# Latents' attention over a context: a new order of transposes, divisions and value products within a batch

## The chip, the cores and the metric

The kernel runs on one core of a Trainium2 chip. The core has five engines that work side by side: TensorE (PE in the profile; its weight loads are listed as PEld), VectorE (DVE), ScalarE (ACT), GpSimd (POOL) and SyncE (SP), which only issues transfers here. Each engine takes its instructions in order, and an instruction waits on semaphores for what other engines produce. The metric is the time of one execution on the device, in microseconds; the lower the better.

## The reference, cut to what matters

The whole kernel is a network of twelve blocks in float32 on x of 16 x 64 tokens by 256. The change is in the tenth block, an attention of the latents (the layer-normed x) over a context of 1024 tokens and over the latents themselves, with a mask on the context:

```python
xn = layernorm(x, ln_x_g, ln_x_b)              # the context, 16 x 1024 x 192
ln = layernorm(latents, ln_l_g, ln_l_b)        # 16 x 64 x 256
q = ln @ Wq.T
kv = jnp.concatenate([xn @ Wkv.T, ln @ Wlkv.T], axis=1)
k, v = (kv[..., :INNER], kv[..., INNER:])      # INNER = 256: 4 heads of 64
...
qn = rmsnorm(q, qn_g) * SCALE
kn = rmsnorm(k, kn_g)
attn = jnp.einsum('bhid,bhjd->bhij', qn, kn)
attn = jnp.where(full_mask[:, None, None, :], attn, -jnp.finfo(attn.dtype).max)
attn = jax.nn.softmax(attn, axis=-1)
out = jnp.einsum('bhij,bhjd->bhid', attn, v)
out = out.transpose(0, 2, 1, 3).reshape(b, m, INNER)
return out @ Wo.T + bo
```

## The kernel before, in words

The block is `xattn3` (L1448 on). It loops over the 16 batches of 64 queries each. The four heads are two pairs, c = 0 and 1, and a pair's scores lie in one tile of 128 rows (two heads by 64 queries) and 1152 keys: 1024 of the context and 128 columns for the latents, half of them masked. Softmax runs along these 1152 keys.

The loop is pipelined over two batches. While batch b is scored, divided and multiplied with its values, the keys and values of batch b + 1 are made. They come in four pieces of 256 context keys (`project`, L1553): products on PE, then four evictions by DVE that apply the context's normalisation, two for keys (`kk`) and two for values (`vv`). Each piece's keys then need their own norm: `square` on ACT, `roots` (a sum by DVE, and two POOL instructions, L1522 and L1523), `scale` on DVE, and `keys_T` (L1583): four transposes on PE into one PSUM accumulator and one copy from there to `kT`. The latents' own keys and values (`latents`, L1538) are a product for two batches at once, so it runs in every second batch; the keys go the same way through square, roots and scale.

For batch b itself: `scores` on PE for the first 512 keys, for the latents' and for the other 512; `least` on DVE adds the mask and keeps the running minimum (the gain has a negative sign); one exponential on ACT per pair gives probabilities `prs[c]` and their sums; a reciprocal on DVE and a multiplication on ACT divide them. Then the probabilities are transposed, eight blocks of a pair by `probs_T` (L1624, two accumulators, two ACT copies into `pT`) and the latents' block of both pairs by `last_T` (L1593), which in this version also transposes the latents' keys of the next batch in the same accumulator. `values` (L1631) multiplies 36 small products per pair into one accumulator `po`, ACT copies `po` to `oT`, and every second batch `output` (L1643) multiplies the output weights for an earlier pair of batches and DVE adds the result to X.

What sets the order is the text of the loop. Between `set_order(True)` and `set_order(False)` every instruction on PE, and every one issued through the wrapped `dve` and `act` queues, is chained to the one before it on its engine, so these three engines run in just the order in which the loop's lines stand. POOL's instructions and the transfers are placed by a scheduler. In the profile the chained DVE and ACT instructions all carry the line of the wrapper, L72, products L188 and transposes L191, so a reader tells them apart by tile names: `pkv` a projection, `ptk` a piece's key transposes, `ptl` those of `last_T`, `ptp` those of `probs_T`, `pss` scores, `po` values or output, `rnk` the norm's sums and roots.

PSUM holds seven accumulators for all of these (`mid`) and one for `po`. The first batch's keys are made ahead of the loop; batches 1 to 3 also make the queries of four later batches each (`queries`, `queries_T`), and batch 0 normalises the second half of the latents.

Of the kernel before, what the change touches and what calls it, by code (L numbers as in the profile page):

```python
# [8 lines left out]
F32 = mybir.dt.float32  # L9
# [6 lines left out]
P = 128  # L16
# [3 lines left out]
S, C = 1024, 192  # L20
C1 = C - P
NKC = S // P
# [56 lines left out]
class Net:  # L79
# [1368 lines left out]
    def xattn3(self):  # L1448
# [9 lines left out]
        H, KT = 4, NKC + 1  # L1458
# [4 lines left out]
        with ExitStack() as es:  # L1463
# [2 lines left out]
            dram = es.enter_context(tc.tile_pool(name=f"{L}dram", bufs=1, space=bass.MemoryType.DRAM))  # L1466
            mid = es.enter_context(tc.tile_pool(name=f"{L}mid", bufs=7, space=PSUM))
            ps_o = es.enter_context(tc.tile_pool(name=f"{L}ps_o", bufs=1, space=PSUM))
            if not hasattr(self, "wx"):
                self.context_weights()(mid)  # L1470
            wx, bx = self.wx, self.bx


# [37 lines left out]
            def square(x, n):  # L1511

                sq = two.tile([P, 2 * H, 64], F32, tag="sq", name="sq")
                act.activation(sq[:, : n * H].rearrange("p (j h) d -> p j h d", j=n), x, AF.Square)
                return x, n, sq

            def roots(x, n, sq):

                rn = self.small.tile([P, 2 * H], F32, tag="rnk", name="rnk", bufs=6)
                r = rn[:, : n * H]  # L1520
                dve.tensor_reduce(r, sq[:, : n * H], AX.X, ALU.add)
                nc.gpsimd.tensor_scalar(r, r, 1.0 / 64, 1e-16, ALU.mult, ALU.max)  # L1522
                nc.gpsimd.tensor_tensor(r, r, self.mhalf[:, : n * H], ALU.pow)  # L1523
                return x, r.rearrange("p (j h) -> p j h", j=n)

            def scale(x, r):
                dve.tensor_tensor(x, x, bc(r, 3, 64), ALU.mult)
# [25 lines left out]
            def project(b, j):  # L1553

                c0, c1 = ctxs[b]
                kk, vv = kks[b % 2], vvs[b % 2]
                pp = [mid.tile([P, 512], F32, tag="m", name="pkv") for _ in range(2)]
                for n in range(2):
                    jj = 4 * n + j
                    self.mm(pp[n], c0[:, jj * P : (jj + 1) * P], wx[:, 0, :], True, False)  # L1560
                for n in range(2):
                    r = slice(n * 64, (n + 1) * 64)
                    self.mm(pp[n], c1[r, j * P : (j + 1) * P], wx[r, 1, :], False, True)
                for n in range(2):
                    for i, dst in enumerate((kk, vv)):
                        jj = 4 * n + j
                        dve.scalar_tensor_tensor(
                            dst[:, 2 * j + n].rearrange("p h d -> p (h d)"),
                            pp[n][:, i * D : (i + 1) * D],
                            self.rctx[:, b, jj : jj + 1],  # L1570
                            bx[:, i * D : (i + 1) * D],
                            ALU.mult,
                            ALU.add,
                        )
                return kk[:, 2 * j : 2 * j + 2], 2

            def turn(pt, at, x):
                self.tr(pt[:, at * P : (at + 1) * P], x)

            def pair(b, k, c):  # L1580
                return kks[b % 2][:, k, 2 * c : 2 * c + 2, :].rearrange("p h d -> p (h d)")

            def keys_T(b, j, copy):  # L1583

                if j == 0:
                    st["kT"] = one.tile([P, 2, KEYS], F32, tag="kT", name="kT")
                pt = mid.tile([P, 512], F32, tag="m", name="ptk")
                for c in range(2):
                    for n in range(2):
                        turn(pt, 2 * c + n, pair(b, 2 * j + n, c))  # L1590
                copy(st["kT"][:, :, 2 * j * P : 2 * j * P + 2 * P], pt.rearrange("p (c k) -> p c k", c=2))

            def last_T(b, keys, prs):  # L1593

                pt = mid.tile([P, 512], F32, tag="m", name="ptl")
                if keys:
                    for c in range(2):
                        turn(pt, c, pair(b, NKC, c))
                if prs:
                    st["pT"] = one.tile([P, 2, KT, P], F32, tag="pT", name="pT")  # L1600
                    for c in range(2):
                        turn(pt, 2 + c, prs[c][:, S:])
                    act.copy(st["pT"][:, :, NKC, :], pt[:, 2 * P :].rearrange("p (c q) -> p c q", c=2))
                if keys:
                    act.copy(st["kT"][:, :, S:], pt[:, : 2 * P].rearrange("p (c k) -> p c k", c=2))

            def scores(b, lo, hi):

# [15 lines left out]
            def probs_T(c, pr):  # L1624
                for jh in range(2):
                    pt = mid.tile([P, 512], F32, tag="m", name="ptp")
                    for j in range(4):
                        turn(pt, j, pr[:, (4 * jh + j) * P : (4 * jh + j + 1) * P])
                    act.copy(st["pT"][:, c, 4 * jh : 4 * jh + 4, :], pt.rearrange("p (j q) -> p j q", q=P))
# [79 lines left out]
            p0 = roots(*p0)  # L1709
# [17 lines left out]
            late = square(*late)  # L1727
            scale(*lat)
            keys_T(0, 2, act.copy)
            last_T(0, True, None)  # L1730
            late = roots(*late)
            scale(*late)
            norm(1)
            for b in range(B):
                more = b + 1 < B
                load(b + 2)
                load_off(b + 1)
                prs = [two.tile([P, KEYS], F32, tag="pr", name="pr") for _ in range(2)]
                nms = [3e38, 3e38]
                sums = self.small.tile([P, 2], F32, tag="sums", name="sums")  # L1740
                st["po"] = ps_o.tile([P, 2 * TQ], F32, tag="o", name="po")
                pss = scores(b, 0, 512)
                for c in range(2):
                    least(b, pss, 0, 512, prs, nms, c)
                keys_T(b, 3, act.copy)
                if more:
                    lat = latents(b + 1)
                    p0 = square(*project(b + 1, 0))
                    lat = square(*lat)
                psl = scores(b, S, KEYS)  # L1750
                pss = scores(b, 512, S)
                for c in range(2):
                    least(b, psl, S, KEYS, prs, nms, c)
                    least(b, pss, 512, S, prs, nms, c)
                    act.activation(prs[c], prs[c], AF.Exp, bias=nms[c], scale=-1.0, accum_out=sums[:, c : c + 1])
                if more:
                    p0, lat = roots(*p0), roots(*lat)
                    p1 = project(b + 1, 1)
                    scale(*p0)
                dve.reciprocal(sums, sums)  # L1760
                if more:
                    p1 = square(*p1)
                act.mul(prs[0], prs[0], sums[:, 0:1])
                if more:
                    p1 = roots(*p1)
                if 1 <= b <= 3:
                    q = queries(b)
                if b == 0:
                    normed(1)
                if more:  # L1770
                    p2 = project(b + 1, 2)
                    scale(*p1)
                    scale(*lat)
                    if b == 0:
                        norm_T(1)
                    keys_T(b + 1, 0, act.copy)
                act.mul(prs[1], prs[1], sums[:, 1:2])
                if 1 <= b <= 3:
                    q = roots(*q)
                if more:  # L1780
                    p2 = roots(*square(*p2))
                    late = project(b + 1, 3)
                last_T(b + 1, more, prs)
                probs_T(0, prs[0])
                if more:
                    late = square(*late)
                    keys_T(b + 1, 1, dve.tensor_copy)
                    late = roots(*late)
                    scale(*p2)
                if 1 <= b <= 3:  # L1790
                    scale(*q)
                probs_T(1, prs[1])
                values(b, 0)
                if more:
                    keys_T(b + 1, 2, dve.tensor_copy)
                if 1 <= b <= 3:
                    queries_T(b, q[0])
                if b % 2 == 0 and b > 0:
                    output(b // 2 - 1)
                values(b, 1)  # L1800
                if more:
                    scale(*late)
                act.copy(oT[:, :, b * TQ : (b + 1) * TQ], st["po"].rearrange("p (c q) -> p c q", c=2))
                if 1 <= b <= NT:
                    nc.gpsimd.tensor_tensor(self.X[:, b - 1, :], self.X[:, b - 1, :], row, ALU.add)
# [771 lines left out]
```

## Time and profile before

| | |
|---|---|
| median of three runs | 3303.53 us |
| lowest and highest | 3290.88 and 3317.2 us |
| the profiled execution: time | 3300.39 us |
| the profiled execution: span | 3298.7 us |
| mean granted TensorE clock over the span | 0.959 |
| busy PE / DVE / ACT / POOL over the span | 94 / 56 / 37 / 22 % |
| the latents' attention's batches | about 2622 to 3007 us |

The span runs from the first to the last instruction; the time has 1.7 us more around it. A row of a group gives line, engine, operation, the tile written and the tiles read, shapes and the number of instructions; then busy time. In a timeline the first two numbers are start and length in us, and a bracket tells how long the engine was idle before and which instruction released it. A row of a stretch gives each engine's busy time with its count of instructions, then the granted clock of TensorE (1.00 is full speed), the share of busy DMA engines and GB/s. A row of waits gives who waited for whom, us in total, times, and the longest.

### The profile page before, as it was taken

What the parts mean: (1) busy time and instruction counts of PE and PEld (TensorE: products, weight loads), DVE (VectorE), ACT (ScalarE), POOL (GpSimd) and SP (SyncE); (2) the same over time, 40 slices, a digit from 0 to 9 for tenths busy, and PEclk for the clock granted to TensorE, in tenths of its full rate; (3) what the DMA queues carried; (4) which work ended last, traced back from release to release, by engine and by line L of the source; (5) the groups of instructions that cost most, each with busy time, mean ns of one, the idle gap of its engine ahead of it and who ended that gap; (6) DMA issues with size and microseconds to landing.
All of it is one profiled execution on the core that took longest, in us unless ns stands there. A gap on an engine that the chain in (4) does not pass through costs nothing.

```text
span 3298.7 us, 48631 instructions
## 1 busy us (share of the span) xinstructions
PE 3085.0 (94%) x20064; PEld 1753.1 (53%) x20064; DVE 1857.1 (56%) x3497; ACT 1213.9 (37%) x2093; POOL 723.5 (22%) x786
## 2 busy tenths in 40 slices
PE   7999999999999999979969999998999899998787
PEld 4666665664344344468834434434665454455676
DVE  6888885424444445961135545557884677775521
ACT  3555554213322221003322232228861254544211
POOL 1000003311200001014410000023771354441131
PEclk9999999999999999969989999998998999999889
DMA  2100000012122113027821111101111111110233
GB/s 71 32 29 30 31 24 11 20 48 79 58 76 73 59 38 78 20 84 288 294 89 58 49 52 54 48 17 34 45 52 34 64 61 55 58 51 14 83 110 118
DMA packets 64511, 213.63 MB, mean 65 GB/s; under 512 B 16433, under 2 KB 27556, under 8 KB 57378
## 3 DMA queue, kind: packets, MB, share of 16 engines
q1 hardware_dynamic: 37296, 106.13, 9.6%
q0 software_dynamic: 21840, 99.39, 9.0%
q10 hardware_dynamic: 5154, 5.01, 0.5%
q8 instruction: 159, 2.61, 0.3%
q14 instruction: 62, 0.51, 0.1%
HBM read 201.62 MB, written 12.66 MB: 65 GB/s over the span
## 4 chain that ended last, share of the span: by engine, by line
PE 78%; DVE 8%; issue 5%; POOL 5%; ACT 3%; DMA 1%; POOLq 0%; DVEq 0%; SPq 0%; ACTq 0%
PE pss L188 14%; PE o L188 13%; PE pst L191 8%; PE pu L188 6%; PE psp L188 5%; PE pd L188 5%; PE py L188 4%; PE psc L188 3%; POOL rnk L1523 2%; PE po L188 2%; PE pb L191 2%; PE psq L188 1%; PE pkv L188 1%; DVE pr L72 1%; DVE kk L72 1%
## 5 line engine op out<-in xcount | busy, mean ns | idle before, releaser
L72 DVE TENSOR_REDUCE nm<-pss 128x1 f32<-128x1024 f32 x256 | 307.4, 1222 | 349.6 <-PE pss L188 349.6
L72 ACT COPY pT<-pst 128x512 f32<-128x512 f32 x256 | 149.8, 585 | 688.8 <-PE pst L191 688.5
L188 PE MATMUL pss<-cT,qw 128*128 128x512 f32 (+1 forms) x1024 | 387.8, 628 | 1.6 <-ACT qw L72 1.6
L188 PE MATMUL o<-pT,cx 128*128 128x512 f32 (+1 forms) x1024 | 370.5, 606 | 0.0
L191 PEld LDWEIGHTS pst<-ident,pr 128*128 128x128 f32 x2048 | 219.8, 141 | 159.1 <-issue 100.1
L72 ACT ACTIVATE pr<-pss,nm 128x1024 f32<-128x1024 f32 x256 | 285.1, 1114 | 34.4 <-DVE nm L72 21.0
L191 PE MATMUL pst<-ident,pr 128*128 128x128 f32 x2048 | 281.0, 280 | 5.7 <-DVE v L72 1.6
L188 PEld LDWEIGHTS pss<-cT,qw 128*128 128x128 f32 (+1 forms) x1024 | 125.8, 187 | 251.1 <-issue 239.4
L188 PEld LDWEIGHTS o<-pT,cx 128*128 128x128 f32 (+1 forms) x1024 | 112.6, 162 | 166.3 <-issue 145.0
L72 DVE TENSOR_SCALAR pr<-pr,sm 128x1024 f32<-128x1024 f32 x256 | 193.1, 754 | 9.0
L188 PE MATMUL pkv<-wx,cT 128*128 128x512 f32 (+1 forms) x512 | 190.2, 623 | 0.6 <-issue 0.6
L205 POOL TENSOR_SCALAR rs<-mv 128x8 f32<-128x8 f32 (+3 forms) x53 | 10.2, 193 | 802.3 <-DVE mv L221 400.3
L72 DVE COPY pT<-pst 128x512 f32<-128x512 f32 x256 | 174.5, 682 | 8.6 <-PE pst L191 4.5
L72 DVE TENSOR_TENSOR_SCAN h<-dA,pb 128x512 f32<-128x512 f32 x128 | 154.7, 1217 | 15.9 <-PE pb L191 9.0
L1347 POOL TENSOR_TENSOR h<-h,cb 128x1024 f32<-128x1024 f32 x64 | 151.4, 2367 | 53.3 <-DVE h L72 51.3
L188 PE MATMUL pd<-wd,hT 128*128 128x256 f32 x656 | 149.3, 382 | 3.0 <-DVE hT L2391 1.4
L2203 DVE TENSOR_SCALAR y<-pd,row 128x256 f32<-128x256 f32 x39 | 18.9, 484 | 223.7 <-PE pd L188 223.7
L188 PEld LDWEIGHTS pd<-wd,hT 128*128 128x128 f32 x656 | 123.1, 190 | 31.3 <-DVE hT L2391 6.2
L1523 POOL TENSOR_TENSOR rnk<-rnk,mhalf 128x8 f32<-128x8 f32 (+1 forms) x84 | 130.2, 1550 | 7.0
L188 PE MATMUL py<-h,ident 128*128 128x512 f32 x256 | 131.1, 598 | 0.0
L188 PEld LDWEIGHTS pu<-xT,up 128*128 128x128 f32 x736 | 110.8, 192 | 21.8 <-ACT hT L2197 14.6
L188 PE MATMUL pu<-xT,up 128*128 128x128 f32 x736 | 121.2, 290 | 1.1 <-DVE xT L2189 0.5
(511 smaller groups left out, 5195.6 us busy)
## 6 DMA issues: line engine op xcount, KB each, us to landing
cT<-in_ctxT SPq DMA_DIRECT2D x64, 768.0 KB, 4.4
cx<-in_ctxP SPq DMA_DIRECT2D x32, 768.0 KB, 4.3
offb<-d_off SPq DMA_DIRECT2D x16, 576.0 KB, 3.7
cb<-d_C SPq DMA_DIRECT2D x16, 512.0 KB, 3.6
wu<-in_L_ffn_w POOLq DMA_DIRECT2D x8, 1024.0 KB, 5.7
wd<-in_L_ffn_w POOLq DMA_DIRECT2D x8, 1024.0 KB, 6.3
wc<-in_L_attn_conv_wT POOLq DMA_DIRECT2D x4, 1024.0 KB, 10.2
T<-d_T SPq DMA_DIRECT2D x8, 512.0 KB, 18.5
```

The lines of the kernel that those rows point to most:

```text
L72: ins = getattr(self.engine, op)(*args, **kwargs)
L188: self.in_order(self.nc.tensor.matmul(out, lhsT=lhsT, rhs=rhs, start=start, stop=stop))
L191: self.in_order(self.nc.tensor.transpose(out, in_, self.ident))
L205: nc.gpsimd.tensor_scalar(t[:p, :n], in_, scale, eps, ALU.mult, ALU.add)
L1347: nc.gpsimd.tensor_tensor(hs[i], hs[i], cbs[hf, g], ALU.mult)
L1523: nc.gpsimd.tensor_tensor(r, r, self.mhalf[:, : n * H], ALU.pow)
L2203: nc.vector.tensor_scalar(y[:, i, :], po[:, i * D : (i + 1) * D], weight[:, g + i : g + i + 1], None, ALU.mult)
```

## The change: what it does

It rewrites the order within a batch.

- The first piece's key transposes (`keys_T(b + 1, 0)`) move from between the third and fourth projection to behind the fourth and behind the first pair's probabilities.
- `last_T` is split: `latents_T` for the next batch's latents' keys, and `last_T` for the latents' block of the probabilities. Each has its own accumulator and stands at its own place, the keys' one late, ahead of piece 1's transposes.
- The reciprocal of both sums becomes two, one per pair. The first division stands right after the first reciprocal, ahead of piece 1's projection in the text; the second right after piece 1's square.
- Scalings on DVE move: piece 0's behind the second reciprocal, piece 1's behind the fourth piece's eviction.
- The copies of pieces 1 and 2 move from DVE to ACT.
- Both value products stand together; piece 2's transposes, the queries' transposes and the output product come after them.
- A branch that builds the context's weights, if no earlier block has done so, is removed; the ninth block does so (L2354).

```diff
--- before.py
+++ after.py
@@ -1466,8 +1466,6 @@
             dram = es.enter_context(tc.tile_pool(name=f"{L}dram", bufs=1, space=bass.MemoryType.DRAM))
             mid = es.enter_context(tc.tile_pool(name=f"{L}mid", bufs=7, space=PSUM))
             ps_o = es.enter_context(tc.tile_pool(name=f"{L}ps_o", bufs=1, space=PSUM))
-            if not hasattr(self, "wx"):
-                self.context_weights()(mid)
             wx, bx = self.wx, self.bx
 
 
@@ -1590,19 +1588,19 @@
                         turn(pt, 2 * c + n, pair(b, 2 * j + n, c))
                 copy(st["kT"][:, :, 2 * j * P : 2 * j * P + 2 * P], pt.rearrange("p (c k) -> p c k", c=2))
 
-            def last_T(b, keys, prs):
+            def latents_T(b):
 
                 pt = mid.tile([P, 512], F32, tag="m", name="ptl")
-                if keys:
-                    for c in range(2):
-                        turn(pt, c, pair(b, NKC, c))
-                if prs:
-                    st["pT"] = one.tile([P, 2, KT, P], F32, tag="pT", name="pT")
-                    for c in range(2):
-                        turn(pt, 2 + c, prs[c][:, S:])
-                    act.copy(st["pT"][:, :, NKC, :], pt[:, 2 * P :].rearrange("p (c q) -> p c q", c=2))
-                if keys:
-                    act.copy(st["kT"][:, :, S:], pt[:, : 2 * P].rearrange("p (c k) -> p c k", c=2))
+                for c in range(2):
+                    turn(pt, c, pair(b, NKC, c))
+                act.copy(st["kT"][:, :, S:], pt[:, : 2 * P].rearrange("p (c k) -> p c k", c=2))
+
+            def last_T(prs):
+
+                pt = mid.tile([P, 512], F32, tag="m", name="pto")
+                for c in range(2):
+                    turn(pt, c, prs[c][:, S:])
+                act.copy(st["pT"][:, :, NKC, :], pt[:, : 2 * P].rearrange("p (c q) -> p c q", c=2))
 
             def scores(b, lo, hi):
 
@@ -1727,7 +1725,7 @@
             late = square(*late)
             scale(*lat)
             keys_T(0, 2, act.copy)
-            last_T(0, True, None)
+            latents_T(0)
             late = roots(*late)
             scale(*late)
             norm(1)
@@ -1755,49 +1753,55 @@
                     act.activation(prs[c], prs[c], AF.Exp, bias=nms[c], scale=-1.0, accum_out=sums[:, c : c + 1])
                 if more:
                     p0, lat = roots(*p0), roots(*lat)
+                dve.reciprocal(sums[:, 0:1], sums[:, 0:1])
+                act.mul(prs[0], prs[0], sums[:, 0:1])
+                if more:
                     p1 = project(b + 1, 1)
-                    scale(*p0)
-                dve.reciprocal(sums, sums)
+                dve.reciprocal(sums[:, 1:2], sums[:, 1:2])
                 if more:
                     p1 = square(*p1)
-                act.mul(prs[0], prs[0], sums[:, 0:1])
+                act.mul(prs[1], prs[1], sums[:, 1:2])
                 if more:
+                    scale(*p0)
                     p1 = roots(*p1)
                 if 1 <= b <= 3:
                     q = queries(b)
                 if b == 0:
                     normed(1)
                 if more:
-                    p2 = project(b + 1, 2)
-                    scale(*p1)
+                    p2 = square(*project(b + 1, 2))
                     scale(*lat)
                     if b == 0:
                         norm_T(1)
-                    keys_T(b + 1, 0, act.copy)
-                act.mul(prs[1], prs[1], sums[:, 1:2])
                 if 1 <= b <= 3:
                     q = roots(*q)
                 if more:
-                    p2 = roots(*square(*p2))
+                    p2 = roots(*p2)
                     late = project(b + 1, 3)
-                last_T(b + 1, more, prs)
+                st["pT"] = one.tile([P, 2, KT, P], F32, tag="pT", name="pT")
                 probs_T(0, prs[0])
                 if more:
+                    keys_T(b + 1, 0, act.copy)
+                last_T(prs)
+                if more:
                     late = square(*late)
-                    keys_T(b + 1, 1, dve.tensor_copy)
+                probs_T(1, prs[1])
+                if more:
+                    scale(*p1)
                     late = roots(*late)
                     scale(*p2)
+                    latents_T(b + 1)
+                    keys_T(b + 1, 1, act.copy)
                 if 1 <= b <= 3:
                     scale(*q)
-                probs_T(1, prs[1])
                 values(b, 0)
+                values(b, 1)
                 if more:
-                    keys_T(b + 1, 2, dve.tensor_copy)
+                    keys_T(b + 1, 2, act.copy)
                 if 1 <= b <= 3:
                     queries_T(b, q[0])
                 if b % 2 == 0 and b > 0:
                     output(b // 2 - 1)
-                values(b, 1)
                 if more:
                     scale(*late)
                 act.copy(oT[:, :, b * TQ : (b + 1) * TQ], st["po"].rearrange("p (c q) -> p c q", c=2))
```

## The prediction

> **What bounds the kernel now.** I read the page first, then the stretches of the latents' attention, its waits, and the timeline of two of its batches.
>
> ```profile
> span 3298.7 us, 48631 instructions
> PE 3085.0 (94%) x20064; PEld 1753.1 (53%) x20064; DVE 1857.1 (56%) x3497; ACT 1213.9 (37%) x2093; POOL 723.5 (22%) x786
> ```
>
> TensorE (PE) is busy nearly throughout. The changed stage is 16 batches, from about 2622 to 3007 us, 12% of the span. One batch with the latents' product and one without, with columns PE, PEld, DVE, ACT, POOL and the granted clock:
>
> ```profile
> 2798.10:2822.40 24.30, 22.60 (x174) 11.45 (x176) 16.79 (x43) 12.11 (x21) 10.91 (x13) 1.00 0.17 57
> 2822.40:2845.70 23.30, 21.61 (x172) 11.20 (x172) 17.95 (x44) 11.52 (x20) 10.49 (x11) 1.00 0.19 60
> ```
>
> PE fills all but 1.7 us of each. [...] in the timeline the 512-column passes of a projection follow each other every 0.43 us (0.19 us of weight load, 0.24 us of PEld idle behind it), without a wait on another engine. The waits of PE itself in these two batches are what an order can remove:
>
> ```profile
> PE ptl L191 <- DVE kk L72: 1.9, 2, 0.9
> PE ptk L191 <- DVE sums L72: 1.0, 2, 0.5
> PE ptk L191 <- DVE kk L72: 0.5, 2, 0.3
> ```
>
> Together 3.4 us in two batches, 1.7 us in each, the same 1.7 us as 24.30 - 22.60. The timeline shows where:
>
> ```profile
> 2811.92 0.63 PE L191 MATMUL ptk<-ident,kk 128*128 128x128 f32 x4 [0.48 <-DVE sums L72]
> ...
> 2813.40 1.66 POOL L1523 TENSOR_TENSOR rnk<-rnk,mhalf 128x8 f32<-128x8 f32 x1
> ...
> 2815.09 1.03 DVE L72 TENSOR_TENSOR kk<-kk,rnk 128x512 f32<-128x512 f32 x2 [1.10 <-POOL rnk L1523]
> ...
> 2816.27 0.41 PE L191 MATMUL ptl<-ident,kk 128*128 128x128 f32 x2 [0.94 <-DVE kk L72]
> ...
> 2818.24 0.69 DVE L72 COPY kT<-ptk 128x512 f32<-128x512 f32 x1
> ...
> 2820.55 0.63 PE L191 MATMUL ptk<-ident,kk 128*128 128x128 f32 x4 [0.27 <-DVE kk L72]
> ```
>
> Piece 0's transposes come between the third and fourth projection, 0.48 us too early for their scaling. The latents' transposes wait 0.94 us because DVE scales piece 1 first, and that waits for a POOL root. Piece 2's transposes wait 0.27 us.
>
> **The change, part by part.** I lay the new order onto this batch, counting from its first score product (2798.08 = 0), with each duration from the timeline. Up to the exponentials nothing changes: last score minima at 10.13, piece 1's products start at 7.34.
>
> *PE.* Each projection takes 2.97 us (weight loads from 2805.42 to 2808.39), and now three follow without a gap: 7.34, 10.31, 13.28, end 16.25. Their accumulators come free in time: a pool of seven gives the fourth piece those of scores read by 10.1. Then comes one row of 28 transposes at 0.13 us (8 took 1.04): first probabilities to 17.3, piece 0 to 17.8, the latents' probabilities to 18.05, second probabilities to 19.05, latents' keys to 19.3, piece 1. Then both values, 1.2 us each, and piece 2.
>
> *The divisions.* ACT ends both exponentials at 11.66. The first reciprocal (at most the 0.16 us of the present two-column one) runs at 11.14 on DVE, hidden behind the second exponential, so the first division (1.25 us) runs 11.66 to 12.91; square of piece 1 (0.62) to 13.53; second division to 14.78. PE wants them at 16.25 and 17.8: covered by 3 us each. The reciprocal more per batch, 0.16 us of DVE, lies in DVE's chain below.
>
> *DVE, the chain to watch.* From 10.13: two reductions 1.01, reciprocal 0.16, eviction of piece 1 (4 by 0.39) 1.57, reciprocal 0.16; scaling of piece 0 at 13.1 (its POOL root is done at 12.97) to 13.78, reduction (0.67) to 14.45, eviction of piece 2 to 16.0, latents' scaling (0.35) to 16.4. ACT squares piece 2 by 16.4, so DVE reduces it to 17.2, evicts the fourth piece to 18.8 and scales piece 1 only now, to 19.5. PE is at piece 1's transposes at 19.35 and a signal takes 0.14 us: a wait of 0.3 us. That is the new late one. Queued behind it are both values, piece 2 and the next batch's scores. The latents' scaling was done 2.9 us before PE wants it: the 0.94 us is gone. Piece 0 is scaled 3.5 us ahead: the 0.48 us is gone.
>
> *Later steps.* Square of the fourth piece on ACT by 19.6, reduction by 20.4, scaling of piece 2 by 21.1; PE wants it at 22.5: the 0.27 us is gone. POOL's root of the fourth piece is done near 22.5, DVE scales it by 23.25, and the next batch's transposes want it at 23.9. In even batches the addition of the output to X (0.42 us) stands before that scaling, and output is now the last thing on PE: X and scaling end 1.25 us after output, PE arrives after 1.02 us of scores. I take 0.3 us of new wait in every second batch.
>
> *Copies.* Pieces 1 and 2 move from DVE (2 by 0.69) to ACT (2 by 0.58): ACT 12.1 to 13.3 of some 23 us. Between 17 and 21.7 ACT works without a gap; the second probabilities' copies are done at 20.7, their values start at 21.3. Covered with 0.6 us; if ACT were later, each us would stop the second values.
>
> *No cost.* Separating the two halves of one accumulator adds no instruction, only an accumulator of the seven. The removed branch is never taken, since an earlier block sets these weights. No DMA is moved; the context's load waits for the fourth projection, which now ends 1 us sooner in the batch. POOL keeps its five roots of 0.25 + 1.66 us or less, under 12 of 23 us.
>
> *What has no row.* Whether 28 transposes in a row hold the clock. [...] the new row lasts 3.6 to 4 us, today's longest some 2.7. This trace has a row that speaks more strongly:
>
> ```profile
> 3001.00:3002.00 1.00, 1.00 (x6) 1.00 (x6) 0.00 (x0) 0.58 (x1) 0.00 (x0) 0.50 0.00 0
> 3002.00:3002.50 0.50, 0.50 (x5) 0.50 (x3) 0.00 (x0) 0.41 (x1) 0.00 (x0) 0.50 0.00 0
> 3002.50:3003.00 0.50, 0.50 (x10) 0.29 (x11) 0.00 (x0) 0.35 (x2) 0.00 (x0) 0.97 0.00 0
> ```
>
> In the last batch, after 6 us of idle PE, only transposes run from 2999.1 to 3002.7, and at its end the clock is back at full. So they count: zero by the row. [...] with the transposes at the slow 0.21 us of that stretch another 28 x 0.08 = 2.2 us. Below nothing it can't go: the clock is at 1.00 already.
>
> **The sum.** Batches 4 to 14: 1.7 - 0.3 - 0.15 = 1.25 us each, 13.7. Batches 1 to 3 have the queries' product and lengths of 25.97, 25.11 and 26.73 us between first scores; products of 24.7, 23.9 and 24.7 (the steady 22.55 or 20.8, 0.9 for output, 2.2 for queries) leave 4.4 idle, and I take 4.1 of it, since DVE's chain has the queries' 1.7 us on PE as cover. Batch 0: PE waits for the normalised latents as before (1.4 us), later waits of some 1.7 us go, one new appears: 0.8. Last batch: division starts 0.2 us sooner, and the first probabilities' transposes no longer stand behind the second division: about 1.1. In all 19.7, say 20 us, of the profiled 3300.4 us (span 3298.7 and 1.7 around it) 0.6%. Applied to the median of 3303.5: 3283.
>
> **The rivals.**
> *DVE's chain takes the place of the removed waits.* Piece 1's scaling behind the fourth eviction has 0 us of margin. If each of DVE's dozen steps starts 0.1 us later than I laid it, it is 1.2 us later, the batch keeps a wait of 1.5 us and little is left: about 1 us in the edges and batches 1 to 3 most of 4: 3298. For it: DVE has hardly a gap from 10.1 to 19.5. Against: the steps' starts are read from the trace, with their gaps.
> *Slower: the clock falls in the row of transposes.* [...] The three rows above speak against it.
> *More than forecast.* Neither new wait appears and the contiguous values pack closer: all 1.7 us in 11 batches, 4.4, 2 in batch 0 and 2 in the last, 27 us: 3276. More than that the stage doesn't hold as idle PE.
>
> **Chances.** Forecast 0.60 (3277 to 3290), DVE's chain 0.20 (3290 to 3303), more 0.13 (3268 to 3277, with the scatter of a median), slower by the clock 0.07. About 1% is what a measurement can tell from no change here, since the three times span 0.8%. The range 3268 to 3303 takes the first three with some scatter out at either end. Faster by over 1% needs 33 us, more than the idle PE in the stage, so only scatter gives it: 0.08. Slower by over 1% [...]: 0.05. The rest, 0.87, is within 1%.
>
> **What would show it.** The period of two steady batches falls from 47.6 to about 45.1 us; the waits of the latents' keys on DVE and of piece 0 vanish from PE's list; a wait of piece 1's transposes on DVE's scaling of about 0.3 us appears; in every second batch one of the fourth piece's transposes behind output; the stage's granted clock stays 1.00. I am wrong if piece 1's wait is over 1 us (DVE), if the second values wait for ACT's copies, or if the clock in the stretch of transposes drops.

## The result, and the profile after

The changed kernel takes 3270.5 us (median of 20 runs, 3262.9 to 3292.6), the kernel before 3293.9 (median of 20, 3288.1 to 3321.9): a ratio of 0.9925 with a 95% interval of 0.9905 to 0.9946, or 23 us (18 to 31 by the interval). The profiled execution went from 3300.4 to 3274.8 us. The forecast was 20 us less, to 3283 us.

The page of the changed kernel, its span and the busy shares:

```profile
span 3273.1 us, 48693 instructions
PE 3078.7 (94%) x20064; PEld 1750.0 (53%) x20064; DVE 1837.4 (56%) x3483; ACT 1228.6 (38%) x2123; POOL 727.5 (22%) x786
```

PE's share is the same 94%, so the page alone shows nothing of where the time went. The stretches of two steady batches do, one with the latents' product and one without (columns as before: PE, PEld, DVE, ACT, POOL, granted clock, DMA share, GB/s):

```profile
2786.71:2809.50 22.79, 22.53 (x170) 11.33 (x169) 16.42 (x44) 12.26 (x21) 10.94 (x14) 1.00 0.18 61
2809.50:2831.20 21.70, 21.64 (x169) 11.21 (x168) 15.61 (x40) 13.18 (x24) 10.71 (x11) 1.00 0.20 65
```

They took 24.30 and 23.30 us before. PE's work is the same; its 1.7 us of idle time per batch is now 0.26 and 0.06. PE's own waits over batches 5 to 14 of the changed kernel are a single row, where the kernel before had three (1.7 us per batch):

```profile
PE ptk L191 <- PE pss L188: 0.9, 5, 0.2
```

This is the wait, in every second batch, of the next batch's last key transposes. The row names the scores, but DVE's scaling ends just then. Batch 4 has one wait more, of 0.48 us, for a scaling that comes late behind the last queries. The timeline of one batch of the changed kernel shows where the old waits were and the two new ones (start, length, what; in brackets the idle time ahead of it):

```profile
2786.82 0.42 DVE L72 TENSOR_TENSOR X<-X,po 128x256 f32<-128x256 f32 x1 [2.90 <-PE po L188]
2787.16 0.69 DVE L72 TENSOR_TENSOR kk<-kk,rnk 128x512 f32<-128x512 f32 x1
...
2787.99 0.63 PE L191 MATMUL ptk<-ident,kk 128*128 128x128 f32 x4 [0.19 <-PE pss L188]
...
2794.28 8.99 PE L188 MATMUL pkv<-wx,cT 128*128 128x512 f32 x24
...
2803.20 1.09 PE L191 MATMUL ptp<-ident,pr 128*128 128x128 f32 x8
...
2805.27 0.69 DVE L72 TENSOR_TENSOR kk<-kk,rnk 128x512 f32<-128x512 f32 x1
...
2805.65 0.38 PE L191 MATMUL ptl<-ident,kk 128*128 128x128 f32 x2
...
2806.10 0.63 PE L191 MATMUL ptk<-ident,kk 128*128 128x128 f32 x4
...
2806.66 2.32 PE L188 MATMUL po<-pT,vv 128*64 128x64 f32 x72
```

Three projections run as one piece of 8.9 us, followed without a gap by the row of transposes. Piece 1's (`ptk` at 2806.10) start 0.45 us after the latents' two, which take 0.22: a wait of 0.23 us. DVE ends the scaling that they need at 2805.96, and its signal takes 0.14. The list of PE's waits doesn't have this one, since the modelled end of the transposes ahead covers most of it. The output's addition to X and the scaling behind it end at 2787.85, and the transposes at 2787.99 wait for them: 0.19 us by the list.

I measure the stage from the start of its first score product to the start of its last output product: 383.5 us before, 364.7 changed. That is 18.9 us of the span's 25.6. The other 6.7 us lie outside it.

### The profile page after: what moved, and what is told of

Its sections match the earlier page's. It is cut to its first block, busy times and chain, and to the rows that moved or that the text cites. A ratio compares the mean times of both kernels' runs of the same rounds, so it can differ in the third digit from the quotient of the medians.

```text
span 3273.1 us, 48693 instructions
## 1 busy us (share of the span) xinstructions
PE 3078.7 (94%) x20064; PEld 1750.0 (53%) x20064; DVE 1837.4 (56%) x3483; ACT 1228.6 (38%) x2123; POOL 727.5 (22%) x786
## 4 chain that ended last, share of the span: by engine, by line
PE 84%; DVE 6%; issue 4%; POOL 2%; ACT 2%; DMA 1%; ACTq 0%; SPq 0%; POOLq 0%; DVEq 0%
PE pss L188 15%; PE o L188 13%; PE pst L191 8%; PE pu L188 6%; PE psp L188 5%; PE pkv L188 5%; PE pd L188 5%; PE py L188 4%; PE psc L188 3%; PE po L188 2%; PE pb L191 2%; PE psq L188 2%; PE psi L188 1%; PE psy L188 1%; PE psqw L188 1%
## 5 line engine op out<-in xcount | busy, mean ns | idle before, releaser
L2207 DVE TENSOR_SCALAR y<-pd,row 128x256 f32<-128x256 f32 x39 | 18.9, 484 | 223.9 <-PE pd L188 223.9
L188 PEld LDWEIGHTS pkv<-wx,cT 128*128 128x128 f32 (+1 forms) x512 | 64.4, 189 | 118.5 <-issue 92.2
## 6 DMA issues: line engine op xcount, KB each, us to landing
wc<-in_L_attn_conv_wT POOLq DMA_DIRECT2D x4, 1024.0 KB, 10.8
```

Of the source, the lines that this page charges most:

```text
L188: self.in_order(self.nc.tensor.matmul(out, lhsT=lhsT, rhs=rhs, start=start, stop=stop))
L2207: nc.vector.tensor_scalar(y[:, i, :], po[:, i * D : (i + 1) * D], weight[:, g + i : g + i + 1], None, ALU.mult)
```

## The experiments

All compare two steady batches (first score product to the first score product two batches later; 47.59 us before, 44.48 changed), the sum of batches 1 to 3, which also make queries, and the stage. Whole times of single runs scatter too much for this. The stage also holds the first and the last batch, whose length depends on where the clock falls in that profile (below), so a difference of one to three us between two stages says little by itself. In a_only, keys0_early, copies_dve and dve_late, the rows of waits are over eight steady batches.

| kernel (all in us) | two steady batches | batches 1 to 3 | stage |
|---|---|---|---|
| before | 47.59 | 77.81 | 383.5 |
| changed | 44.48 | 73.31 | 364.7 |
| a_only | 47.59 | 78.00 | 386.2 |
| keys0_early | 45.52 | 73.73 | 369.8 |
| p1_scaled_first | 47.31 | 75.32 | 382.1 |
| long_transposes | 50.97 | 83.25 | 416.4 |
| values_apart | 44.54 | 75.78 | 365.8 |
| copies_dve | 44.97 | 74.70 | 368.2 |
| one_division | 44.48 | 73.29 | 364.7 |
| dve_late | 45.69 | 75.04 | 372.7 |
| three_parts | 44.54 | 77.57 | 368.3 |
| warm_clock | 44.48 | 73.30 | 362.9 |
| warm_and_order | 44.35 | 73.84 | 358.4 |
| after_again | 44.48 | 73.29 | 364.7 |

**One move alone (a_only).** On the kernel before:

```diff
-                    keys_T(b + 1, 0, act.copy)
                 act.mul(prs[1], prs[1], sums[:, 1:2])
...
                     late = project(b + 1, 3)
+                    keys_T(b + 1, 0, act.copy)
                 last_T(b + 1, more, prs)
```

> The kernel before with one part of the change: piece 0's key transposes and their copy stand behind the fourth projection instead of ahead of it. Two steady batches took 47.6 us before and take 44.5 us changed. My theory, that the waits come from the order of scalings on DVE and from POOL's root: the 0.48 us wait at piece 0 goes, but the latents' transposes still need DVE's scaling of piece 1 and then of the latents, which comes no sooner, so their wait grows from 0.94 to about 1.4 us, and two batches stay at 47.6 (47.4 to 47.8). Rival, that each removed wait is a gain by itself: two batches fall by 2 x 0.48 to 46.7.

47.59 us, to the hundredth what it was. PE's waits over eight steady batches of this kernel:

```profile
PE ptl L191 <- DVE kk L72: 10.1, 8, 1.3
PE ptk L191 <- DVE kk L72: 2.2, 8, 0.3
```

The wait at piece 0 is gone and the latents' has grown from 0.94 to 1.3 us a batch. A removed wait is worth nothing while the next one on the same engine hangs on the same chain.

**That move undone (keys0_early).** On the changed kernel:

```diff
                     if b == 0:
                         norm_T(1)
+                    keys_T(b + 1, 0, act.copy)
...
                 probs_T(0, prs[0])
-                if more:
-                    keys_T(b + 1, 0, act.copy)
```

> The changed kernel with piece 0's transposes and copy back between the third and fourth projection. My theory: PE is there at about 13.5 us of the batch, and the scaling of piece 0, now behind two reciprocals, ends at 13.9 and is signalled 0.14 later, so a wait of 0.5 us comes back; the wait of 0.2 us at piece 1 goes in exchange, two batches take 45.1 (44.9 to 45.6) against 44.5. Rival, that the place of piece 0 doesn't matter because DVE's chain sets the batch: 44.5.

45.52: undoing the move loses 0.52 us a batch, where alone the move gained nothing. Its waits over eight batches:

```profile
PE ptk L191 <- DVE kk L72: 3.8, 8, 0.5
PE ptk L191 <- PE pss L188: 0.8, 4, 0.2
```

0.48 us each, at piece 0. The loss is at the upper end of what I expected.

**Piece 1's scaling put back (p1_scaled_first).**

```diff
                     p2 = square(*project(b + 1, 2))
+                    scale(*p1)
                     scale(*lat)
...
                 if more:
-                    scale(*p1)
                     late = roots(*late)
```

> The changed kernel with DVE's scaling of piece 1 back ahead of the latents' scaling, ahead of piece 2's reduction and the fourth piece's eviction; nothing else is moved. My theory: DVE waits there for piece 1's POOL root (about 0.6 us) and everything behind it, the fourth eviction, its square and its root, comes 0.6 to 1.1 us later; the second probabilities need the accumulator of the fourth piece, and the next batch's last transposes need its scaling, so two batches lose 0.8 to 2 us: 45.3 to 46.5. Rival, that separating the latents' transposes is what gained and the place of this scaling is free: 44.5, or 44.1 since the wait of 0.2 us at piece 1 goes.

47.31: this one line takes back 2.8 of the 3.1 us, more than I expected. Its timeline:

```profile
2813.15 1.66 POOL L1521 TENSOR_TENSOR rnk<-rnk,mhalf 128x8 f32<-128x8 f32 x1
...
2814.85 1.03 DVE L72 TENSOR_TENSOR kk<-kk,rnk 128x512 f32<-128x512 f32 x2 [1.17 <-POOL rnk L1521]
...
2816.78 0.47 DVE L72 SCALAR_TENSOR_TENSOR vv<-pkv,rctx,bx 128x256 f32<-128x256 f32 x1
...
2817.40 0.63 PE L191 MATMUL ptp<-ident,pr 128*128 128x128 f32 x4 [1.14 <-DVE vv L72]
```

DVE stands 1.17 us, not 0.6, behind POOL's root with the fourth piece's eviction queued behind it. The second half of the second probabilities' transposes needs the accumulator that this eviction frees, and PE waits 1.14 us for it. Without the new place of this scaling, all the rest of the change, the latents' separate transposes with it, gains 0.3 us in two batches; the rival falls.

**The row of transposes, longer (long_transposes).**

```diff
                 for c in range(2):
                     turn(pt, c, prs[c][:, S:])
+                for n in range(32):
+                    turn(pt, 2 + n % 2, prs[n % 2][:, :P])
```

> The changed kernel with 32 more transposes per batch, of blocks already transposed, into the unused half of the accumulator of the latents' probabilities; their results are not read. The row of transposes between the fourth projection and the values becomes 60 long, about 8 us. My theory, that transposes count as activity for the clock: the granted clock stays 1.00 in that row and a batch grows by 32 x 0.13 = 4.2 us, two batches 44.5 + 8.4 less 0.4 = 52.5. Rival, that they don't count: the clock falls to about half within the row, transposes take 0.21 us, and two batches take 56 us or more.

50.97: 3.24 us more a batch, less than I expected. The transposes follow each other at 0.11 us (34 from 2821.58 to 2825.29), not the 0.13 that I took from a group of eight with its tail: 3.5 us, less the wait at piece 1 that they cover. The clock is the eighth number of these rows:

```profile
2821.00:2822.00 1.00, 1.00 (x11) 1.00 (x10) 1.00 (x4) 1.00 (x3) 0.89 (x2) 1.00 0.51 123
2824.00:2825.00 1.00, 1.00 (x12) 1.00 (x11) 0.00 (x0) 0.00 (x0) 0.00 (x0) 1.00 0.05 18
2826.00:2827.00 1.00, 1.00 (x12) 0.83 (x11) 0.56 (x1) 1.00 (x3) 0.00 (x0) 1.00 0.00 0
```

From 2820.2 to 2826.9, 6.7 us, PE does transposes only, and the granted clock stays 1.00, here and in the score products behind (every us from 2820 to 2845). The slower rival of the prediction is out.

**The values apart (values_apart).**

```diff
                 values(b, 0)
-                values(b, 1)
...
                     output(b // 2 - 1)
+                values(b, 1)
```

> The changed kernel with the two value products apart again: piece 2's transposes, the queries' and the output product stand between them. Theory A, that bringing both values together removed the wait of piece 2's transposes: the 0.27 us come back, two batches take 45.0. Theory B, that DVE's scaling of piece 2 is now ready before the first values end (by 0.3 us in the changed kernel's trace): no wait returns, and the output's addition to X is no longer late, so the 0.19 us at the next batch's last transposes goes: 44.3.

44.54, between the two. No wait of PE is left in its list, so theory B is right on both waits. But the values joined take 2.25 us from the first of them to the next transposes (2806.66 to 2808.91 in the changed kernel), apart 1.20 each. The joined values are worth 0.15 us a batch, a little more than the late addition to X costs (0.2 us in every second batch). In batches 1 to 3 keeping them apart costs 2.5 us: piece 2's scaling comes later there, behind the queries' reduction and root.

**The copies on DVE (copies_dve).**

```diff
-                    keys_T(b + 1, 1, act.copy)
+                    keys_T(b + 1, 1, dve.tensor_copy)
...
-                    keys_T(b + 1, 2, act.copy)
+                    keys_T(b + 1, 2, dve.tensor_copy)
```

> The changed kernel with the copies of pieces 1 and 2 back on DVE. My theory: ACT gets shorter by 1.2 us and DVE longer by 1.4; piece 2's copy stands ahead of the fourth piece's scaling on DVE, which ends 0.6 us later, so the next batch's last transposes wait 0.5 us more in batches with output and not in the others: two batches 45.0 (44.7 to 45.4). Rival, that ACT without a gap behind the probabilities was the tighter one: at most 44.5.

44.97, with a wait of 0.5 us in every second batch, as laid out; its list over eight batches:

```profile
PE ptk L191 <- DVE kk L72: 1.8, 4, 0.5
PE ptk L191 <- PE pss L188: 0.8, 4, 0.2
```

**One late division (one_division).**

```diff
-                dve.reciprocal(sums[:, 0:1], sums[:, 0:1])
-                act.mul(prs[0], prs[0], sums[:, 0:1])
                 if more:
                     p1 = project(b + 1, 1)
-                dve.reciprocal(sums[:, 1:2], sums[:, 1:2])
+                dve.reciprocal(sums, sums)
                 if more:
                     p1 = square(*p1)
+                act.mul(prs[0], prs[0], sums[:, 0:1])
                 act.mul(prs[1], prs[1], sums[:, 1:2])
```

> The changed kernel with one reciprocal of both sums behind piece 1's eviction and both divisions on ACT behind piece 1's square. My theory: both are ready at about 16.1 us of the batch, PE wants the first at 16.5 and the second at 17.8, so the sooner division gains nothing directly; piece 2's square on ACT starts 0.3 us later and takes DVE's chain with it, so two batches take 44.5 to 45.1. Rival, that the sooner divisions are a part of the gain: 46 or more.

44.48, and 73.29 in batches 1 to 3: the sooner divisions are worth nothing measurable there. In the last batch, where no projection covers them, they are: without them the first probabilities' transposes start 10.03 us after the first score, for 9.69 in the changed kernel. The equal stage, 364.7, doesn't show it, since its batch 0 was shorter by about as much (29.3 us for 29.6).

**A step more in DVE's chain (dve_late).**

```diff
+                    dve.tensor_tensor(idle, idle, idle, ALU.mult)
                     scale(*p1)
```

The tile `idle` is made and filled once, ahead of the loop.

> The changed kernel with one more DVE instruction per batch, a multiplication of 128 x 512 numbers that nobody reads (0.6 us of DVE), right ahead of piece 1's scaling. My theory, that DVE's chain there has no margin left: the wait of piece 1's transposes grows from 0.2 to 0.8 us and each batch by 0.6, two batches 45.7. Rival, that DVE has slack because it is busy for only 18 of 22 us: 44.5.

45.69: the 0.6 us cost 0.60 us a batch. DVE has no slack there, though it is busy for under 17 of 22 us. The wait at piece 1 now shows in the list:

```profile
PE ptk L191 <- DVE kk L72: 5.3, 8, 0.7
```

**Three moves of the change (three_parts).** The last three undone together (one division, copies on DVE, values apart), the rest changed. More than three moves are left: piece 0's scaling, piece 2's square and the place of piece 1's transposes behind the second probabilities' also stay as changed, and no run undoes one of these alone.

> The changed kernel with everything as before but three moves: piece 0's transposes behind the fourth projection, the latents' transposes apart and late, piece 1's scaling behind the fourth eviction. The single late division, the copies of pieces 1 and 2 on DVE and the values apart are back. My theory, that these three moves carry the gain: two batches take 45.0 to 45.3, that is 2.3 to 2.6 of the 3.1 us gained. Rival, that the parts need each other: above 46.

44.54, better than expected: all but 0.06 us of the steady gain. The 0.5 us that the copies on DVE cost with joined values is not there when the output stands between the values. In batches 1 to 3, however, next to nothing of the 4.5 us is gained. The timeline of one of them shows why:

```profile
2672.06 0.69 DVE L72 TENSOR_TENSOR kk<-kk,rnk 128x512 f32<-128x512 f32 x1 [0.59 <-POOL rnk L1521]
2672.66 0.68 DVE L72 COPY kT<-ptk 128x512 f32<-128x512 f32 x1
2672.89 0.63 PE L191 MATMUL ptk<-ident,kk 128*128 128x128 f32 x4 [0.73 <-DVE kk L72]
...
2673.27 0.68 DVE L72 TENSOR_TENSOR q<-q,rnk 128x512 f32<-128x512 f32 x1
...
2674.09 0.63 PE L191 MATMUL ptq<-ident,q 128*128 128x128 f32 x4 [0.57 <-DVE q L72]
```

The queries' root makes POOL and DVE late for piece 2, and a copy stands on DVE ahead of the queries' scaling. Joined values give piece 2 1.2 us more; the copies on ACT take the 0.68 us out. Alone, values apart cost 2.5 us in these batches and the copies on DVE 1.4.

**PE kept busy where it idles (warm_clock).** 44 and 48 transposes of the identity that nobody reads, on the changed kernel:

```diff
+            def warm(n):
+                pt = mid.tile([P, 512], F32, tag="m", name="ptw")
+                for k in range(n):
+                    turn(pt, k % 4, self.ident)
...
             keys_T(0, 1, act.copy)
+            warm(44)
             queries_T(0, q[0])
...
+                if not more:
+                    warm(48)
                 probs_T(0, prs[0])
```

> The changed kernel with 44 transposes of the identity, read by nobody, into PE's idle 5.5 us ahead of the first queries' transposes, and 48 into its idle 6 us of the last batch. If transposes hold the clock, it stays at 1.00 through the first batch, which falls from 29.6 to 26 to 27.5 us (from first score product to the next batch's), and the last batch falls from 17.1 to 15 to 15.6 us. If they don't, both stay within 0.3 us. Two steady batches stay at 44.5.

Half right. The last batch falls from 17.1 to 14.7 us, more than I expected. The first doesn't fall (30.3): PE is done with its first scores sooner, only to wait longer for the fourth piece's scaling (3.06 us for 2.14 in the changed kernel), and the clock still drops behind that wait (granted 0.50 from 2634.6 to 2636.6):

```profile
2632.75 0.63 PE L191 MATMUL ptk<-ident,kk 128*128 128x128 f32 x4 [3.06 <-DVE kk L72]
2633.21 4.59 PE L188 MATMUL pkv<-wx,cT 128*128 128x512 f32 x8
```

At a granted clock of 1.00 a projection takes 2.94 us (2649.93 to 2652.87 in the changed kernel).

**And a better order (warm_and_order).** In addition:

```diff
                     least(b, pss, 0, 512, prs, nms, c)
+                if b == 0:
+                    normed(1)
                 keys_T(b, 3, act.copy)
...
-                if b == 0:
-                    normed(1)
...
                     latents_T(b + 1)
-                    keys_T(b + 1, 1, act.copy)
                 if 1 <= b <= 3:
                     scale(*q)
                 values(b, 0)
+                if more:
+                    keys_T(b + 1, 1, act.copy)
+                if b % 2 == 0 and b > 0:
+                    output(b // 2 - 1)
                 values(b, 1)
                 if more:
                     keys_T(b + 1, 2, act.copy)
                 if 1 <= b <= 3:
                     queries_T(b, q[0])
-                if b % 2 == 0 and b > 0:
-                    output(b // 2 - 1)
```

> As the one before, and in addition: the first values stand ahead of piece 1's transposes and the output product between the values, and batch 0 normalises the second half of the latents ahead of its late scores. My theory: the two waits left over, 0.19 us at piece 1 and 0.19 us at the next batch's last transposes, go, two batches take 43.9 to 44.1; the first batch loses its wait of 1.9 us for the normalised latents; the stage from its first score product to the last output product takes 364.7 - 3 - 5 - 2 = 355 us (352 to 358), the kernel some 8 to 10 us less than the changed one, 3261. Rival, that the clock in other stages scatters by more than this: the stage falls all the same, the time can't be told from the changed kernel's.

The stage falls by 6.3 us to 358.4, just outside what I expected (355, at most 358): 2.6 from the first batch (29.6 to 27.0) and 3.3 from the last. PE has no wait left in the steady batches, yet they take 44.35, not 43.9 to 44.1: the values are apart again. The time, 3267.3 us (median of 6, 3264.2 to 3274.2), can't be told from the 3269.6 us (3265.1 to 3274.5) of the changed kernel in the same rounds, as the rival had it; its ratio to the kernel before is 0.9898 (0.9856 to 0.9939).

**The changed kernel once more (after_again).** No edit.

> The changed kernel as it is, in the same rounds. Its stage takes 364 to 366 us as in its first profile if the stage's gain of 18.9 us doesn't depend on the run; what the first profile gained beyond that, 6.7 us outside the stage, is the run's scatter and needn't return: the time lies 17 to 27 us under the kernel before.

The stage takes 364.7 again, to 0.04 us. Its time is 3269.6 us (median of 6) against 3298.1 (median of 11) for the kernel before: 0.9900 (0.9858 to 0.9941). That is 28.5 us less, a little beyond the 17 to 27 that I expected.

## Why the prediction was right

The difference of 20 us was right within its error; the mechanism was right where most of the gain lies, in the steady batches. The absolute figure was less good. 3270.5 us lies outside the 3277 to 3290 of the forecast, in the band that the prediction kept for closer packing (chance 0.13). That is mainly the starting point: the prediction took off 20 from a median of three runs, 3303.5, and the median of twenty is 3293.9.

That the sum came so close is in part luck: of its 19.7 us the stage gave 18.9, because the steady batches gave 3.0 us more, batches 1 to 3 gave 0.4 more, and the two ends together 4.2 less.

- **Steady batches, 1.25 us each: 1.51 each, 16.7 in eleven batches for 13.7.** Both new waits were named and came at their places, 0.23 us at piece 1 for 0.3, and 0.19 in every second batch for 0.3. The wait of 0.48 us in batch 4 was not foreseen. The rest, some 0.15 us a batch, the sum didn't have: two joined values take 2.25 us, not twice 1.2. The prediction held that closer packing for a rival.
- **What removes the waits.** The prediction told each move by itself. The experiments show that they act together: piece 0's place alone gains nothing, and without the new place of piece 1's scaling 2.8 of 3.1 us are lost.
- **Covers at zero cost.** The divisions: right in the steady batches, their sooner place gains nothing. The copies on ACT: covered as said, and needed because the output's addition is late. Accumulators: right in this order, but with piece 1 scaled first it is just the fourth piece's accumulator that PE waits for.
- **Batches 1 to 3: 4.5 us for 4.1.** Here the joined values (2.5 us) and the copies (1.4) matter, which the steady batches don't show.
- **Batch 0: a loss of 2.2 us for a gain of 0.8.** Most of this is the clock. In the profile of before the first projection of this batch ran at a granted clock of 1.00. In a_only the clock was at 0.50 from 2631.3 to 2633.3, in the changed kernel from 2622 to 2624.5. In the order before, a_only, changed:

```profile
2626.04 2.94 PE L188 MATMUL pkv<-wx,cT 128*128 128x512 f32 x8
2630.49 4.59 PE L188 MATMUL pkv<-wx,cT 128*128 128x512 f32 x8
2621.26 4.59 PE L188 MATMUL pkv<-wx,cT 128*128 128x512 f32 x8
```

  The kernel a_only has the same instructions up to there as the kernel before, yet it had the slow projection and 29.9 us in batch 0, where the one profile of before had 27.45. In all thirteen other profiles this projection takes 4.59 us, only in before's 2.94. So the 2.2 us are the luck of that profile. Against a_only the changed kernel gains 0.3 us in batch 0, and 21.5 in the stage, nearer to the 23 of the medians. One term was wrong beside the clock: PE waits 1.91 us for the normalised latents, where the prediction kept the 1.4 of the kernel before (1.38 in a_only too).
- **Last batch: a loss of 0.15 us for a gain of 1.1.** The first probabilities' transposes do come ahead of the second division: they start 9.7 us after the first score, where those of the kernel before start at 10.8. But the first division starts 0.3 us later, not 0.2 sooner: the exponential ahead of it starts 0.5 us later, behind the late output's addition and the next block's statistics on DVE. In values_apart, where the output isn't late, the transposes start at 9.0. The rest is the clock, granted 0.50 in the changed kernel's transposes and in its values up to 2979, 0.54 from there to 2980, then 1.00. The same instructions, starting at the same times up to the transposes, went faster in keys0_early: its values took 2.32 us, as long as those of before, where the clock was at 0.97 as they began and 1.00 after. The 72 products of the values, changed and keys0_early:

```profile
2978.40 3.00 PE L188 MATMUL po<-pT,vv 128*64 128x64 f32 x72
2978.32 2.32 PE L188 MATMUL po<-pT,vv 128*64 128x64 f32 x72
```

  The last batch took 17.1 us in the changed kernel and 16.0 in keys0_early, for 16.9 in the one profile of before. So this loss, too, is partly luck, and what the change is worth here at equal clock stays open.
- **Outside the stage, nothing: 6.7 us.** The stage's code is the only one that differs. Span less stage lies between 2897.7 us (copies_dve, mean granted clock 0.963) and 2932.6 (dve_late, 0.952) in these profiles, so 6.7 us is within the scatter of runs.

Of the rivals, DVE's chain was the true danger: 0.6 us more in it costs 0.6 us a batch. In the changed kernel it is late by no more than the 0.23 us at piece 1. The clock's fall in the row of transposes did not come; by the prediction's estimate it would have made a batch's 28 transposes 2.2 us longer (0.21 us each, as at 0.50 in the last batch of before, for 0.13). The prediction's three rows of the last batch, 0.50 in the transposes and 0.97 at their end, spoke against it, and 6.7 us of these float32 transposes at a granted clock of 1.00 (long_transposes) confirm them.

## What to carry to other kernels

On an engine that runs in a written order, count a wait as gained only after laying the whole next cycle out: a removed wait falls into the next one on the same chain, and a move that is worth nothing alone can be worth half a us a batch beside the others. Scale or evict last what is wanted last, and don't put a step that waits for a slow engine ahead of one that frees an accumulator. Judge such an edit by the steady cycle in the trace, which here repeats to a few hundredths of a us, when the whole time scatters by 1%. Before calling a change in the first or last cycle a gain or a loss, compare profiles whose instructions are the same there: the clock may have fallen at another place, as it did here for the first projection of batch 0 (2.94 us in before, 4.59 in a_only).

## What the runs showed of the hardware that I had not expected

- Transposes alone kept the clock up where PE would otherwise idle: in warm_clock, with 44 unread ones in PE's idle 5.5 us ahead of the first batch, the granted clock was 1.00 in every us from 2621.6 to 2626.6, where in the changed kernel it was 0.50 from 2612.1 to 2614.1, in that idle time. With 48 in PE's idle 6 us the last batch took 14.7 us instead of 16.0 to 17.2 (six profiles with the same instructions there).
- In warm_clock the clock fell behind 3.1 us of idle PE in the first batch (granted 0.72, 0.50, 0.50 and 0.58 in the four us from 2633.6); in the changed kernel it fell so behind idle times of 2.1 and 1.9 us, when PE was already busy again (granted 0.50 from 2622 to 2624.5 and from 2635.5 to 2638.5).
- Identical code met such a fall in one profile and not in another: the first projection of batch 0 took 2.94 us in the one profile of before and 4.59 in a_only.
- The same 36 products of 64 columns twice took 2.25 us in one row (changed) and 1.20 us each in two (values_apart). Four transposes took 0.56 us with such products behind them (from 2806.10, changed), and 0.44 with more transposes behind (from 2804.12).
